# Twelve tiles instead of four leave PSUM by ACT and get tokens and bias by accumulating transfers

## The chip, the core and the metric

The kernel runs on one core of one Trainium2 chip. The metric is the device time of one execution in microseconds (us), median of several. A profile is one further execution, recorded by the hardware profiler; its span runs from the first to the last recorded instruction. The engines of a core are PE (matmul), PEld (its weight loads), DVE (vector), ACT (scalar), POOL and SP; each runs its own queue of instructions in order, and DMA transfers are issued from SP's, ACT's and POOL's queues.

## What is computed

x holds 64 batches of 64 tokens by 1024 features. Each batch has a condition, which picks one of 16 matrices of 64x64; the matrix mixes the 64 rows of the batch. On the result a feed-forward layer acts: a base product with a 1024x1024 weight and a bias, plus a low-rank product of 8 experts of rank 16, of which a gate picks the best two. The input is added at the end.

```
W = weights[condition]
h = einsum('bct,bcd->bdt', x, W)
gate_logits = einsum('bsd,ed->bse', h, gate_w)
weights, selected = top_k(gate_logits, 2);  weights = softmax(weights)
result = einsum('bsd,od->bso', h, base_w) + base_b
low = einsum('bsd,erd->ebsr', h, lora_A)
lora_out = einsum('ebsr,eor,bse->bso', low, lora_B, w_full)
return x + result + 2.0 * lora_out
```

## The kernel before

**Tiles.** The 4096 token rows are 32 tiles of 128 rows, two batches each. The condition matrix mixes rows only and the weights mix columns only, so the kernel multiplies by the weights first and by the condition matrix afterwards. The columns of the joined weight (128 of lora_A, 8 of the gate, 1024 of the base) are three chunks, c = 0, 1, 2, of 384, 388 and 388 columns. The 1024 rows of the weight are four blocks of 256, so that the blocks are named b11 to b43 (row block, then chunk).

**Precision.** Every operand is split into a rounded high part and the rest, and each product is three matmuls: high by high, high by rest, rest by high. The high part is a copy (L234, mostly on ACT): wh of the weights, xh of x, zh of the products, bdh of the condition matrix, lth of the transposed low-rank part. The rest is a subtraction on DVE (L231): wl, xl, zl, bdl, ltl. The subtraction needs the copy, and the matmuls need both.

**Plain tiles and pairs.** Tiles 0 to 3 are multiplied block by block (`plain`): for tiles 0 and 1, row block by row block as the weights arrive, chunks 0 and 1 of both tiles, then chunk 2. Tiles 4 to 31 go in pairs through a scheme with 20 products p1 to p20 in place of 24, on sums and differences of blocks (`Pair.product`), with PSUM banks z0 to z3. The products' matmuls are L414.

**After a product chunk.** `post` brings the chunk z of a tile through the condition matrix: matmuls with bdh and bdl into a bank a0 or a1 (chunk 0) or o0 or o1 (L447). The condition matrix of a tile comes by a gather from HBM, issued from POOL (`load_cond`, L394, tile bdr), and is then split by ACT into bdh and by DVE into bdl. Chunk 0 also feeds the gate (copy low, then small steps L486 to L493 on DVE and ACT) and a transpose of the weighted low-rank part on PE (L500), which is split into lth and ltl; three more matmuls by lora_B add it to every chunk.

**The end of a tile.** `finish` takes each of the three chunks out of PSUM into the tile's buffer xtok, of which there are three, used in turn (tile i uses i % 3). For tiles from 4 on the buffer already holds x + bias, and DVE adds the bank to it (L457). That is the work of `load_tok`: SP loads the tile's x (L380), then POOL issues a transfer of the bias that accumulates onto it (L381). For tiles 0 to 3 ACT copies the bank into the buffer (L234), and `late_sum` afterwards issues from POOL two accumulating transfers onto it, x and then the bias (L388). The store is issued from POOL for tiles 0 to 29 (L464). A transfer onto a buffer waits for the landing of the one before; that wait stands in the issuing engine's queue.

**Order.** No engine's order is written out by hand. Each step is registered with `add`, with the engine, a cost, what it reads and writes, and for matmuls a due time. `Program.run` works back from the due times along the dependences to a latest start of each step (`late`), and then plays the program forward on its costs; whenever an engine is free it takes, among the steps that are ready by that reckoning, the one with the earliest latest start. A DMA enters with its issue, 2.0 us, and its bytes at 360 GB/s, one after another; an accumulating transfer counts 2.5 times its bytes, a gather the 64 KB of its matrix. The order found in this way is then fixed in the queues, whatever the chip's own times are. So a change of what one step costs or waits for can move any other step on any engine.

**The start.** 39 small matmuls on zeros (L225) keep PE busy until the first weights are there. ACT and DVE split the weight blocks (wh_b.., wl_b..) and the x blocks of tiles 0 and 1 (xh, xl) as SP's loads land. The indices of the conditions come by a POOL DMA (L223), POOL makes rows of them (L593), and then issues the first two gathers.

Of the kernel before, what the change touches and what calls it, by code (L numbers as in the profile page):

```python
# [36 lines left out]
NPAIR = NT // 2  # L37
NPLAIN = 2
TOP = 3.0e38
NWARM = 39  # L40

PE, ACT, DVE, POOL, SP = "PE", "ACT", "DVE", "POOL", "SP"
# [37 lines left out]
class Program:  # L80
# [7 lines left out]
    def add(self, engine, cost, fn, reads=(), writes=(), due=None, first=False, size=0.0, early=None, port=False,  # L88
            after=0.0):

        n = len(self.steps)
        engine, cost = (e if isinstance(e, (list, tuple)) else [e] for e in (engine, cost))
        deps = set()
        for b in list(reads) + list(writes):
            if b in self.writer:
                deps.add(self.writer[b])
        for b in writes:
            deps.update(self.readers.get(b, ()))  # L100
        for b in reads:
            self.readers.setdefault(b, []).append(n)
        for b in writes:
            self.writer[b], self.readers[b] = n, []
        deps.discard(n)
        self.steps.append(dict(eng=dict(zip(engine, cost)), fn=fn, deps=deps, first=first, size=size, port=port,
                               lag=FLIGHT + QUEUE + size * DMA if size else 0.0, after=after,
                               due=self.horizon if due is None else due,
                               early=SP in engine and not reads if early is None else early))
# [59 lines left out]
def cond_ffn_kernel(ctx, tc, xT, x, idx, cw, wall, bias, lb, out):  # L169
# [50 lines left out]
    for t in low:  # L220
        nc.vector.memset(t[:, NG:], TOP)
    idx_sb = sb.tile([P, NT], I32, name="idx_sb")
    nc.gpsimd.dma_start(idx_sb, idx)  # L223
    for _ in range(NWARM):
        nc.tensor.matmul(bank["o1"][:, :P], wz, wz, start=True, stop=True)  # L225
# [7 lines left out]
    def copy(e, o, a):  # L233
        (nc.scalar.copy if e == ACT else nc.vector.tensor_copy)(o, a)  # L234
# [139 lines left out]
    def tok_keys(j):  # L374
        return [("xtok", j, str(c)) for c in (0, 1, 2) + PARTS]

    def load_tok(i):
        j = i % 3
        keys = tok_keys(j)
        add(SP, ISSUE, lambda e: nc.sync.dma_start(xtok[j], x[i * P:(i + 1) * P, :]), writes=keys, size=4.0 * T * P)  # L380
        add(POOL, 1.1, lambda e: nc.gpsimd.dma_start(xtok[j], bias.broadcast_to([P, T]), accum_op=ALU.add),  # L381
            writes=keys, size=TWICE * 4.0 * T * P)

    def late_sum(i):

        j = i % 3
        for src in (x[i * P:(i + 1) * P, :], bias.broadcast_to([P, T])):
            add(POOL, 1.1, lambda e, src=src: nc.gpsimd.dma_start(xtok[j], src, accum_op=ALU.add),  # L388
                writes=tok_keys(j), size=TWICE * 4.0 * T * P)

    def load_cond(i):

        j = i % 2
        add(POOL, 1.04, lambda e: nc.gpsimd.indirect_dma_start(  # L394
            out=bdr[j], out_offset=None, in_=cw,
            in_offset=bass.IndirectOffsetOnAxis(ap=rows[:, i:i + 1], axis=0)),
            ["rows"], [("bdr", j)], size=4.0 * P * P, early=True)
        add(ACT, 0.28, lambda e: copy(e, bdh[j], bdr[j]), [("bdr", j)], [("bdh", j)])
        add(DVE, 0.25, lambda e: sub(e, bdl[j], bdr[j], bdh[j]), [("bdr", j), ("bdh", j)], [("bdl", j)], port=True)
# [19 lines left out]
    def split_z(n, src, key):  # L419

        q = take("zq", NZ)
        h, l = zh[q][:, :n], zl[q][:, :n]
        add(ACT, 0.2 + 0.00085 * n, lambda e: copy(e, h, src()), [key], [("zh", q)])
        add(DVE, 0.09 + 0.00104 * n, lambda e: sub(e, l, src(), h), [key, ("zh", q)], [("zl", q)],
            port=isinstance(key, tuple))
        return q

    def outs(c):

        c, p = c if isinstance(c, tuple) else (c, slice(0, CN[c]))  # L430
        lo, o, n = max(OUTS[c][0] - p.start, 0), OUTS[c][2] + max(p.start - OUTS[c][0], 0), p.stop - p.start
        return n, slice(lo, n), slice(o, o + n - lo), p
# [18 lines left out]

    def finish(i, c, b):
        (_, s, o, _), j = outs(c), i % 3
        if i < 2 * NPLAIN:
            return add(ACT, 0.2 + 0.00085 * (s.stop - s.start), lambda e: copy(e, xtok[j][:, o], bank[b][:, s]),
                       [b], [("xtok", j, str(c))])
        add(DVE, 0.09 + 0.00104 * (s.stop - s.start), lambda e: nc.vector.tensor_tensor(  # L457
            xtok[j][:, o], bank[b][:, s], xtok[j][:, o], ALU.add), [b], [("xtok", j, str(c))])

    def store(i, cs):  # L460
        o, j = slice(outs(cs[0])[2].start, outs(cs[-1])[2].stop), i % 3
        src = [("xtok", j, str(c)) for c in cs]
        if i < NT - 2:
            add(POOL, 1.0, lambda e: nc.gpsimd.dma_start(out[i * P:(i + 1) * P, o], xtok[j][:, o]), src,  # L464
                size=4.0 * P * (o.stop - o.start))
        else:

            q, dma = (ACT, nc.scalar.dma_start) if cs[0] == PARTS[1] else (SP, nc.sync.dma_start)
            add(q, ISSUE, lambda e: dma(out[i * P:(i + 1) * P, o], xtok[j][:, o]), src,
                size=4.0 * P * (o.stop - o.start))  # L470
# [37 lines left out]
    def post(i, c, q):  # L508

        if c == 0:  # L510
            b = held[i] = f"a{i % 2}"
            if i >= NT - 2:
                pr.horizon -= SOONER
            sums(i, 0, b, q, (0, 1, 2), start=True)
            gate(i, b)
            tr(i, b)
            sums(i, 0, b, with_lora=True, stop=True)
            finish(i, c, b)
            if i >= NT - 2:
                pr.horizon += SOONER  # L520
            return
        else:
            b = f"o{take('o', 2)}"
            if i >= NT - 2:
                parts = [(c, b)] if (i, c) != (NT - 2, 2) else list(zip(PARTS, (b, "z3")))
                for c, b in parts:
                    sums(i, c, b, with_lora=True, start=True)
                for c, b in parts:
                    sums(i, c, b, q, (0, 1, 2), stop=True)
                    finish(i, c, b)  # L530
                return
            else:
                sums(i, c, b, q, (0, 1, 2), True, True, True)
        finish(i, c, b)
# [8 lines left out]
    t = 4.9  # L543
# [168 lines left out]
    class Pair:  # L712
# [29 lines left out]
        def chunk(self, i, c, o=None):  # L742

            t = 2 * self.q + i
            if o:
                u = self.at[o]
                post(t, c, split_z(CN[c], lambda: unit(u)[:, :CN[c]], ukey(u)))
                sts.give(u)
            else:
                post(t, c, split_z(CN[c], lambda: bank[BANKS["X"]][:, :CN[c]], BANKS["X"]))  # L750
            self.out.add((i, c))
            if self.q == NPAIR - 1:
                for p in PARTS if (i, c) == (0, 2) else (c,):
                    store(t, (p,))
            elif all((i, c) in self.out for c in range(3)):
                store(t, range(3))

        def product(self, p):
# [49 lines left out]
    def load_pair(q):  # L808
        for i in (2 * q, 2 * q + 1):
            load_cond(i)  # L810
            load_tok(i)

    pairs = {}
    for q, p in ORDER:
        pr.horizon = ends[q] + (LAST if q == NPAIR - 1 else LAG)
        if q not in pairs:
            pairs[q] = Pair(q)
        if (q, p) == (NPLAIN, HEAD[3]):
            load_pair(q)
        pairs[q].product(p)  # L820
        if p == TAIL[-1] and q < NPAIR - 1:

            load_pair(q + 1)
# [40 lines left out]
```

## Time and profile before

| | |
|---|---|
| median of 3 runs | 460.26 us (460.14 to 460.26) |
| profiled execution: time | 460.46 us |
| its span | 458.7 us |
| granted PE clock | 1.0 throughout |
| DMA moved | 75.00 MB, mean 164 GB/s |
| accumulating transfers among them | 32 of bias (28 at L381, 4 at L388) and 4 of x |

The profile's page opens with the busy time of each engine, its share of the span and its instructions. Its 40 slices of the span show busy tenths:

```
PE   8999999999999999999999999999999999999995
DVE  5999997879989788796987979798797988888674
ACT  5864666543736345373543646354454544546331
POOL 3030214121303021220303003030210403103000
```

Further views are asked of the trace: a list of waits (who waited for whom, total, times, longest), a timeline (start, length, engine, line, operation, tiles, and in brackets the idle time before it and what ended it), the busy times of each engine in stretches of time, and the DMA issues with their size and the median time from issue to landing. In names, the text before "<-" is what is written. Numbers of buffers and blocks are left out there, so that wh_b_b is the high part of any weight block used plainly; which one it is follows from the order.

### The profile page before, as it was taken

The numbers are of one execution on the slowest core, as the hardware profiler recorded it, in microseconds if no ns is written. First come the engines' busy times: TensorE is split into PE (matmuls) and PEld (weight loads), VectorE is DVE, ScalarE is ACT, GpSimd is POOL, SyncE is SP. The second block draws the span as 40 slices with busy tenths as digits, with TensorE's granted clock in tenths as the row PEclk, the third lists the DMA queues.
The fourth block names the chain that finished last, engine by engine and source line by source line (L and its number), as shares of the span: only waits on it lengthen the run. The fifth ranks groups of instructions, "written<-read, shape, count | busy, mean of one in ns | idle before, by whom it ended". The sixth has DMA issues, their size and how long they took to land.

```text
span 458.7 us, 7577 instructions
## 1 busy us (share of the span) xinstructions
PE 452.7 (99%) x2621; PEld 449.7 (98%) x2621; DVE 383.5 (84%) x941; ACT 227.2 (50%) x520; POOL 89.6 (20%) x107
## 2 busy tenths in 40 slices
PE   8999999999999999999999999999999999999995
PEld 8999999999999999999999999999999999999995
DVE  5999997879989788796987979789797988888674
ACT  5864666543736345373543646354454544546331
POOL 3030214121303021220303003030210403103000
PEclk9999999999999999999999999999999999999999
DMA  8932748977768462764847456565565746556142
GB/s 279 352 117 47 153 107 198 213 211 202 180 206 202 172 161 87 217 131 163 199 127 202 108 182 148 172 162 133 191 123 185 173 129 193 116 174 149 51 134 91
DMA packets 36229, 75.00 MB, mean 164 GB/s; under 512 B 4432, under 2 KB 22240, under 8 KB 36192
## 3 DMA queue, kind: packets, MB, share of 16 engines
q0 software_dynamic: 10560, 36.72, 33.5%
q1 hardware_dynamic: 25200, 37.32, 25.9%
q10 hardware_dynamic: 432, 0.49, 0.4%
q8 instruction: 20, 0.33, 0.3%
q14 instruction: 17, 0.14, 0.1%
HBM read 57.74 MB, written 16.78 MB: 162 GB/s over the span
## 4 chain that ended last, share of the span: by engine, by line
PE 97%; DMA 1%; DVE 1%; ACT 0%; issue 0%
PE ps_z L414 76%; PE ps_o L447 15%; PE ps_a L447 6%; DMA w_b<-in_w 1%; PE ps_a L500 1%; DVE wl_b_b L231 0%; DVE xtok L457 0%; DVE st L740 0%; ACT wh_b_b L234 0%; DVE xl L231 0%; PE ps_z L447 0%; DVE xh L234 0%
## 5 line engine op out<-in xcount | busy, mean ns | idle before, releaser
L231 DVE TENSOR_TENSOR xl<-xr,xh 128x512 fp32r<-128x512 f32 (+1 forms) x138 | 92.1, 670 | 20.0 <-ACT xh L234 19.8
L414 PE MATMUL ps_z<-wh_t_p,xh 128*128 128x388 f32 (+1 forms) x308 | 105.3, 342 | 0.1
L414 PE MATMUL ps_z<-wh_t_p,xl 128*128 128x388 f32 (+1 forms) x308 | 104.3, 339 | 0.0
L414 PE MATMUL ps_z<-wl_t_p,xh 128*128 128x388 f32 (+1 forms) x308 | 104.3, 339 | 0.0
L234 ACT CAST xh<-xr 128x512 fp32r<-128x512 f32 (+1 forms) x136 | 82.5, 610 | 37.2 <-PE ps_z L414 32.5
L740 DVE TENSOR_TENSOR st<-ps_z,st 128x388 f32<-128x388 f32 x126 | 70.2, 558 | 21.2 <-PE ps_z L414 20.2
L292 DVE TENSOR_TENSOR xr<-xr 128x256 f32<-128x256 f32 (+1 forms) x139 | 69.6, 526 | 3.6 <-DMA xr<-in_xT 3.4
L414 PE MATMUL ps_z<-wh_b_p,xh 128*128 128x388 f32 (+1 forms) x180 | 61.4, 341 | 0.0
L414 PE MATMUL ps_z<-wh_b_p,xl 128*128 128x388 f32 (+1 forms) x180 | 60.9, 338 | 0.0
L414 PE MATMUL ps_z<-wl_b_p,xh 128*128 128x388 f32 (+1 forms) x180 | 60.8, 338 | 0.0
L414 PEld LDWEIGHTS ps_z<-wh_t_p,xh 128*128 128x128 f32 x308 | 57.8, 188 | 1.2 <-DVE st L740 0.7
L414 PEld LDWEIGHTS ps_z<-wl_t_p,xh 128*128 128x128 f32 x308 | 57.9, 188 | 0.0
L414 PEld LDWEIGHTS ps_z<-wh_t_p,xl 128*128 128x128 f32 x308 | 57.9, 188 | 0.0
L464 POOL DMA_DIRECT2D out<-xtok x30 | 16.8, 560 | 193.6 <-DVE xtok L457 89.6
L234 ACT CAST zh<-st 128x388 fp32r<-128x388 f32 (+1 forms) x70 | 36.1, 517 | 22.1 <-DVE st L740 15.2
L381 POOL DMA_DIRECT2D xtok<-in_bias x28 | 27.0, 964 | 96.9 <-DMA xtok<-in_x 89.6
L394 POOL DMA_INDIRECT bdr<-in_cw,rows x32 | 36.9, 1155 | 26.4 <-DVE zl L231 17.7
L457 DVE TENSOR_TENSOR xtok<-ps_o,xtok 128x388 f32<-128x388 f32 (+1 forms) x56 | 30.9, 554 | 11.2 <-PE ps_o L447 10.7
L723 ACT ACTIVATE ps_z<-ps_z 128x388 f32<-128x388 f32 x42 | 20.1, 478 | 40.5 <-PE ps_z L414 39.4
L231 DVE TENSOR_TENSOR zl<-st,zh 128x388 fp32r<-128x388 f32 (+1 forms) x70 | 38.7, 554 | 0.9 <-ACT zh L234 0.6
L414 PEld LDWEIGHTS ps_z<-wh_b_p,xh 128*128 128x128 f32 x180 | 33.8, 188 | 0.2
L414 PEld LDWEIGHTS ps_z<-wl_b_p,xh 128*128 128x128 f32 x180 | 33.8, 188 | 0.0
(143 smaller groups left out, 873.0 us busy)
## 6 DMA issues: line engine op xcount, KB each, us to landing
xr<-in_xT SPq DMA_DIRECT2D x128, 128.0 KB, 3.2
xtok<-in_bias POOLq DMA_DIRECT2D x32, 512.0 KB, 7.1
out<-xtok POOLq DMA_DIRECT2D x30, 512.0 KB, 3.2
xtok<-in_x SPq DMA_DIRECT2D x28, 512.0 KB, 3.6
w_b<-in_w SPq DMA_DIRECT2D x10, 388.0 KB, 5.9
xtok<-in_x POOLq DMA_DIRECT2D x4, 512.0 KB, 6.6
out<-xtok SPq DMA_DIRECT2D x3, 194.0 KB, 2.2
bdr<-in_cw,rows POOLq DMA_INDIRECT x32, 5.3
```

Of the source, the lines that this page charges most:

```text
L231: eng[e].tensor_tensor(o, a, b.bitcast(F32), ALU.subtract)
L234: (nc.scalar.copy if e == ACT else nc.vector.tensor_copy)(o, a)
L292: add(DVE, tt_cost(2 * P * len(os)), lambda e: nc.vector.tensor_tensor(some(xr, os), some(xr, xs), some(xr, ys), f), [("xr", u) for u in s ...
L381: add(POOL, 1.1, lambda e: nc.gpsimd.dma_start(xtok[j], bias.broadcast_to([P, T]), accum_op=ALU.add), writes=keys, size=TWICE * 4.0 * T * P)
L394: add(POOL, 1.04, lambda e: nc.gpsimd.indirect_dma_start(out=bdr[j], out_offset=None, in_=cw, in_offset=bass.IndirectOffsetOnAxis(ap=rows[ ...
L414: nc.tensor.matmul(z, l[:, j, n], w.ap()[:, f, :cols], start=(start and q == 0), stop=(stop and q == 2), skip_group_check=True)
L447: nc.tensor.matmul(d, l, r, start=(start and m == 0), stop=(stop and m == len(mms) - 1), skip_group_check=True)
L457: add(DVE, 0.09 + 0.00104 * (s.stop - s.start), lambda e: nc.vector.tensor_tensor(xtok[j][:, o], bank[b][:, s], xtok[j][:, o], ALU.add), [ ...
L464: add(POOL, 1.0, lambda e: nc.gpsimd.dma_start(out[i * P:(i + 1) * P, o], xtok[j][:, o]), src, size=4.0 * P * (o.stop - o.start))
L500: add(PE, 0.107, lambda e: nc.tensor.matmul(tp, low[i % 2][:, :ER], ident, is_transpose=True, start=False, stop=False, skip_group_check=True),
L723: add(ACT, 0.2 + 0.00085 * W, lambda e: nc.scalar.mul(z[b], z[x], scale), [BANKS[x]], [BANKS[b]])
L740: add(DVE, 0.09 + 0.00104 * W, lambda e: nc.vector.tensor_tensor(unit(u), a(), b(), f), reads, [ukey(u)])
```

## The change

A new constant LATE = 12 replaces 2 * NPLAIN = 4 as the bound in `finish`; the pairs call `late_sum` ahead of the store of a tile below it; and `load_pair` leaves `load_tok` out for such a tile. So tiles 4 to 11 are treated at their end as tiles 0 to 3 are. Tiles 12 to 31 keep the old way.

```diff
+LATE = 12
...
     def finish(i, c, b):
         (_, s, o, _), j = outs(c), i % 3
-        if i < 2 * NPLAIN:
+        if i < LATE:
             return add(ACT, 0.2 + 0.00085 * (s.stop - s.start), lambda e: copy(e, xtok[j][:, o], bank[b][:, s]),
                        [b], [("xtok", j, str(c))])
...
             elif all((i, c) in self.out for c in range(3)):
+                if t < LATE:
+                    late_sum(t)
                 store(t, range(3))
...
     def load_pair(q):
         for i in (2 * q, 2 * q + 1):
             load_cond(i)
-            load_tok(i)
+            if i >= LATE:
+                load_tok(i)
```

Since the planner settles the order, instructions that the diff does not name stand at other places in the queues too: on PE from about 24 us on (its last 700-odd instructions stand as before), on ACT and DVE from about 9 us on, on SP from about 13 us on, and on POOL from the fifth gather on.

## The prediction

> **What bounds the kernel now.** I read the page's busy shares first, then the busy time by stretches, then the list of waits of PE alone, and only then the timelines of single engines at the places where the change reorders work. The busy shares and two of the stretches:
>
> ```profile
> span 458.7 us, 7577 instructions
> PE 452.7 (99%) x2621; PEld 449.7 (98%) x2621; DVE 383.5 (84%) x941; ACT 227.2 (50%) x520; POOL 89.6 (20%) x107
> ...
> 12.00:40.00 28.00, 28.00 (x162) 27.85 (x161) 27.79 (x54) 18.05 (x37) 3.50 (x2) 1.00 0.57 191
> ...
> 240.00:420.00 180.00, 180.00 (x1039) 179.41 (x1038) 151.71 (x384) 87.45 (x206) 37.07 (x41) 1.00 0.60 161
> ```
>
> In the stretches the columns are length, sum, then PE, PEld, DVE, ACT and POOL busy. From 12 to 420 us PE is busy for the whole of every stretch. A busy PE alone proves little, since its matmuls overlap, but starts support it: two 384-column matmuls start 0.17 to 0.18 us apart, and outside the first 12 and the last 20 us I find no gap over 0.1 us between starts beyond that pace. PE's list of waits holds one entry, at the very start:
>
> ```profile
> PE ps_o L225 <- DVE warm L311: 1.1, 1, 1.1
> ```
>
> Two things follow. Freeing DVE, ACT or POOL in the middle gains nothing: PE has no idle time to give back there; what is left is about 0.7 us near 440 to 447 us, where it waits for DVE st L740, and the order of PE's last 700-odd instructions is the same in the changed program. And any stall of PE is lost for good, because no later slack absorbs it. So the question is only whether the new order makes PE wait anywhere.
>
> **The change, part by part: eviction.** Tiles 4 to 11 have three evictions each. DVE loses 16 of 0.554 us (L457, ps_o) and 8 of 0.405 us: 12.1 us. ACT gains 16 copies of 0.483 and 8 of 0.374 us: 10.7 us, on an engine that is half idle. Cost and gain at the end of the chain: 0, covered by PE's own work on both sides. If ACT's cover were gone, a copy would cost at most its 0.48 us.
>
> **The token transfers.** SP loses eight issues of 0.33 us; POOL gains eight of 0.92 us (the median at L388), a total of 7.4 us on an engine with 20% busy. What matters is the chain behind the last eviction of a tile, in POOL's queue: tokens, then bias onto them, then the store, each waiting for the landing of the last. The DMA view gives:
>
> ```profile
> xtok<-in_bias POOLq DMA_DIRECT2D x32, 512.0 KB, 7.1
> out<-xtok POOLq DMA_DIRECT2D x30, 512.0 KB, 3.2
> xtok<-in_x SPq DMA_DIRECT2D x28, 512.0 KB, 3.6
> xtok<-in_x POOLq DMA_DIRECT2D x4, 512.0 KB, 6.6
> ```
>
> That is 6.6 + 7.1 + 3.2 = 16.9 us until the buffer is free, where before the store, the plain load and the bias took 3.2 + 3.6 + 7.1 = 13.9 us between the same two evictions. The Trainium skill ("DMA: Bandwidth & Descriptors", Anatomy of one DMA) gives a transfer on this path about 2.0 us plus its bytes at 436 GB/s, which makes 3.2 us for 512 KB and 9.6 us for the chain; the rows, which accumulate, say twice that for two of the three, and I use the rows. Where is it felt? With three buffers, the second tile of a pair (t7, t9, t11, evicted first) reuses the buffer of the first tile of the pair before (t4, t6, t8, evicted last). Walking POOL's new order with the positions of the sums in PE's new order (at PE's pace, no stall): t4's last eviction near 103 us, its tokens land at 110, its bias at 117, its store at 120.5; t7's first eviction is ready near 123. For t6 to t9 it is 148 against 151, for t8 to t11 175.5 against 178. A slack of 2.5 to 3 us each. Two accumulations under way at once took up to 9 us (around 75 us). With 9 us each the store lands at most 2 us after the eviction is ready, and what waits behind it in ACT's queue, the copy lth of the other tile, is wanted by PE only 2.2 us or more after that point. Value taken: 0; bounds 0 and about 2 us over the three places. Then t13, which loads the old way again behind t10's late store, cannot get its bias before about 213 us; the new order puts its DVE additions behind the sums of the next pair, near 221, so 0 again. Tiles 0 to 3 already run this path in the profile, without a wait of PE.
>
> **The order of the start.** All engines' orders come from a planner, and the eight accumulations lengthen the chain that it works back from. So it moves up the work of the first tiles. ACT's program before and after, from the end of the third weight block (listing, not profile; the names are those of the code):
>
> ```
> before: wh b21, xh, wh b22, xh, wh b31, xh, wh b32, xh, wh b41, xh, bdh0, wh b42
> after:  wh b21, xh, bdh0, wh b22, xh, wh b31, xh, bdh1, wh b32, xh, wh b41
> ```
>
> bdh0 is the copy of the first gathered condition matrix. ACT runs its queue in order, so everything behind it now waits for that gather. On DVE, bdl0 moves up too, ahead of wl b22. POOL's and SP's first issues are the same as before, so the gather comes when it came:
>
> ```profile
> 6.87 1.06 POOL L394 DMA_INDIRECT bdr<-in_cw,rows  x1 [0.18 <-issue]
> ...
> bdr<-in_cw,rows POOLq DMA_INDIRECT x1, 5.9
> ...
> 8.91 0.40 ACT L234 CAST xh<-xr 128x256 fp32r<-128x256 f32 x1
> 9.46 0.84 ACT L234 CAST wh_b_b<-w_b 128x776 fp32r<-128x776 f32 x1
> 10.21 0.40 ACT L234 CAST xh<-xr 128x256 fp32r<-128x256 f32 x1
> ...
> 10.34 0.97 DVE L231 TENSOR_TENSOR wl_b_b<-w_b,wh_b_b 128x776 fp32r<-128x776 f32 x1
> 11.22 0.42 DVE L231 TENSOR_TENSOR xl<-xr,xh 128x256 fp32r<-128x256 f32 x1
> ...
> 11.69 0.44 PE L414 MATMUL ps_z<-wh_b_b,xl 128*128 128x384 f32 x1
> ```
>
> The first row is its issue, the second its time to landing (POOL's DMA issues between 6 and 8 us); then ACT, DVE and PE where the change strikes. It lands at 6.87 + 5.9 = 12.8 us. ACT is free for bdh0 at 8.91 + 0.40 = 9.3. The steps: bdh0 starts at 12.8; in the profile ACT's next instruction started 0.29 us after it (15.12 to 15.41), so wh b22 starts at 13.1 instead of 9.46: 3.6 us late. xh of the second tile follows at 13.8 instead of 10.21, wl b22 on DVE at 13.9 instead of 10.34 (bdl0, 0.27 us, is done by then: hidden), xl at 14.8 to 15.3 instead of 11.22 to 11.64. PE is already at the limit here: in the profile its matmul on xl starts at 11.69, 0.05 us after xl ends, the last of three that use the second tile's block at 11.28, 11.46 and 11.69. It will run dry at about 11.3, get two of them at 14.2 and the third at 15.3. Loss: 15.3 - 11.7 = 3.6 us. It is not made up: PE is full from 12 us on, and what lies behind (DVE 27.79 of 28 us busy) is moved as a whole. ACT wins back its 1.2 us of waits for weights, which now lie ready, against 0.29 us for bdh1, whose gather (issued 8.23) has landed by then. The late weight block b23, whose load waits for a freed buffer, moves with the rest.
>
> The gather's price from both sides: the 32 gathers took 2.5 to 7.3 us to land, so 0 to 5.0 us of stall. By the skill's formula 64 KB would take 2.15 us, land at 9.0, and bdh0 would cost nothing but its 0.29 us. I take 5.9, because it is this very gather, at this place, with the weights' loads around it (they too took 5 to 6 us). The skill also speaks of the PE clock ("TensorE: Matmul & The Clock Gate", The HAM clock gate): about 3.4 us idle halve it. The trace shows only the price: the 39 warm-up matmuls start 107 ns apart for the first 3.9 us, so getting warm again would cost about half of that, 2 us. The expected hole is 14.2 - 11.3 = 2.9 us, under that figure: 0 taken, 2 the upper end.
>
> **Sum.** The profiled execution took 460.46 us, its span 458.7 and 1.8 around it. Span after: 458.7 + 3.6 = 462.3. The median of the runs, 460.26, is 0.2 below the profiled execution; on it, 460.26 + 3.6 = 463.9.
>
> **Rivals.**
> - The hole lets PE's clock fall: 463.9 + 2 = 465.9. For: 2.9 us is near 3.4. Against: it is below, and two matmuls come before the rest of it. 0.13.
> - Late transfers take over: buffers come free after their evictions, ACT waits with lth behind it, and PE stalls at t7, t9, t11 as well: 0.5 to 2 us more, about 465. For: accumulations of 9 us were seen. Against: the slack of 2.5 to 3 us, and tiles 0 to 3. 0.13.
> - Not slower: the gather lands before ACT gets to bdh0. Place: ACT's queue at 9.3 us; price: nothing below a landing time of 2.5 us, less than the 0.2% bound (0.9 us, about what a measurement of this kernel can tell from no change) below some 3.3 us. Then the time is 460.3 to 461.2, since PE's bound stands. For: gathers of 2.5 us exist. Against: those were on quiet queues; the two near the start took 5.9 and 5.4. 0.06, of which 0.01 for faster: by more than 0.9 us it cannot be from PE's remaining gaps, which are about 0.7 us.
> - The forecast, 463.9, itself 463.0 to 464.7 with the gather 0.8 us either way: 0.68.
>
> The range 463.0 to 466.0 takes in the cold clock and most of the late transfers.
>
> **What would show it.** In the changed profile, ACT's bdh has idle time of about 3.4 us before it, released by the DMA bdr, near 12.8 us; PE has a hole of about 3 us before 14.3, released by ACT xh, and a smaller one before 15.3, released by DVE xl; from there to 440 us it is full again, and everything lies 3.6 us later. Matmuls 0.35 us apart after the hole would be the cold clock. Waits of ACT xtok for DMA out near 127, 155 and 182 us, with PE idle after them, would be late transfers. Wrong it is if the gather comes early, or if PE has some slack at 12 us that the trace does not show.

## The result and the profile after

The changed kernel takes **467.35 us** (median of 6 executions, 464.76 to 470.52) against 460.26 us (460.14 to 460.76): a ratio of 1.015 [1.0132, 1.0168], slower by 7.1 us. The forecast was 463.9, with 466.0 as its upper end. The executions of the kernel before lie within 0.6 us; those of the changed one spread over 5.8 us. Part of what happens below is thus different from one execution to the next. The profiled execution was the shortest, 464.76 us with a span of 462.9.

First the page of the changed kernel and its stretches, with the columns as before (length, sum, PE, PEld, DVE, ACT, POOL, granted clock, share of the DMA engines, GB/s):

```profile
span 462.9 us, 7579 instructions
PE 454.3 (98%) x2621; PEld 450.8 (97%) x2621; DVE 373.1 (81%) x917; ACT 234.5 (51%) x544; POOL 94.9 (21%) x115
...
12.00:40.00 28.00, 26.14 (x138) 25.78 (x139) 25.79 (x50) 18.10 (x36) 2.22 (x2) 0.94 0.55 186
212.00:228.00 16.00, 16.00 (x96) 15.98 (x95) 13.65 (x30) 5.90 (x12) 1.46 (x2) 1.00 0.63 169
```

DVE has 10 us less to do, ACT 7 more, and neither shows in the time. In the stretch from 12 to 40 us two things changed: PE has 1.86 us of idle time, where it had none, and the granted clock is 0.94, where it was 1.00. From 212 to 228 us, a place that matters below, PE is full in this execution. PE's list of waits names what it waited for:

```profile
PE ps_z L415 <- ACT wh_b_b L235: 2.5, 1, 2.5
PE ps_o L226 <- DVE warm L312: 1.1, 1, 1.1
PE ps_z L415 <- DVE xl L232: 0.4, 1, 0.4
```

The middle entry was there before. The two others are new, once each. The timelines of ACT and of PE around that place follow, each in a fence of its own (start, length, engine, line, operation, tiles, and the idle time with its releaser). They answer to the rows near 9 to 12 us shown of the kernel before.

```profile
8.48 0.40 ACT L235 CAST xh<-xr 128x256 fp32r<-128x256 f32 x1
12.05 0.30 ACT L235 CAST bdh<-bdr 128x128 fp32r<-128x128 f32 x1 [3.17 <-DMA bdr<-in_cw,rows]
12.26 0.83 ACT L235 CAST wh_b_b<-w_b 128x776 fp32r<-128x776 f32 x1
```

```profile
10.64 0.34 PE L415 MATMUL ps_z<-wh_b_b,xl 128*128 128x384 f32 x1
13.45 0.44 PE L415 MATMUL ps_z<-wh_b_b,xh 128*128 128x384 f32 x1 [2.47 <-ACT wh_b_b L235]
...
14.48 0.44 PE L415 MATMUL ps_z<-wh_b_b,xl 128*128 128x384 f32 x1 [0.41 <-DVE xl L232]
...
15.66 0.52 PE L415 MATMUL ps_z<-wh_b_b,xl 128*128 128x388 f32 x1
15.99 0.53 PE L415 MATMUL ps_z<-wh_b_b,xh 128*128 128x388 f32 x1
```

The first fence and the upper lines of the second are the step that the prediction made: ACT stands at the gather (3.17 us), the weight copy behind it comes late, and so does PE; DVE's xl ends at 14.4, and PE's next start follows at 14.48. Beyond PE's usual pace of 0.175 us from start to start, the hole is 2.6 us at 13.45 and 0.6 at 14.48. Not all of this is loss against the kernel before, since PE came to the hole 0.46 us sooner in this execution (10.64 against 11.10 for the same matmul): behind the hole it is 2.8 us late (14.48 against 11.69).

The last two lines are what the prediction had put at nothing: matmuls of 388 columns that start 0.32 us apart instead of 0.18. Ten of them do, which is 1.5 us. The granted clock, third from the end of each row, is a half over just these matmuls and full in the stretch before them:

```profile
12.18:15.59 3.41, 1.73 (x8) 1.41 (x9) 2.76 (x5) 3.41 (x8) 0.95 (x1) 1.00 1.04 383
15.59:19.01 3.42, 3.42 (x13) 3.42 (x12) 3.42 (x6) 2.58 (x6) 0.00 (x0) 0.50 1.05 372
```

The hole and the slow matmuls make PE 4.3 us late, which is the whole difference of the spans (462.9 against 458.7).

So the shortest execution is explained by the start. The median is 2.6 us longer; for that, another execution is needed (e4 below).

### The profile page after: what moved, and what is told of

Same layout as the page of the kernel before. It is cut to its first block, busy times and chain, and to the rows that moved or that the text cites. A ratio compares the mean times of both kernels' runs of the same rounds, so it can differ in the third digit from the quotient of the medians.

```text
span 462.9 us, 7579 instructions
## 1 busy us (share of the span) xinstructions
PE 454.3 (98%) x2621; PEld 450.8 (97%) x2621; DVE 373.1 (81%) x917; ACT 234.5 (51%) x544; POOL 94.9 (21%) x115
## 2 busy tenths in 40 slices
DMA packets 36230, 75.01 MB, mean 162 GB/s; under 512 B 4432, under 2 KB 22240, under 8 KB 36192
## 4 chain that ended last, share of the span: by engine, by line
PE 96%; DMA 2%; issue 0%; DVE 0%; ACT 0%; POOL 0%; POOLq 0%; DVEq 0%
PE ps_z L415 74%; PE ps_o L448 15%; PE ps_a L448 6%; DMA bdr<-in_cw,rows 1%; DMA idx_sb<-in_idx 1%; PE ps_a L501 1%; ACT wh_b_b L235 0%; DVE xtok L458 0%; DVE st L741 0%; DVE xl L232 0%; POOL rows L594 0%; POOL ident masks.py:199 0%; PE ps_z L448 0%; ACT bdh L235 0%; POOL ident masks.py:197 0%
## 5 line engine op out<-in xcount | busy, mean ns | idle before, releaser
L395 POOL DMA_INDIRECT bdr<-in_cw,rows x32 | 35.5, 1108 | 33.5 <-ACT e L489 17.7
L415 PEld LDWEIGHTS ps_z<-wh_b_p,xl 128*128 128x128 f32 x180 | 33.8, 188 | 0.0
L382 POOL DMA_DIRECT2D xtok<-in_bias x20 | 19.4, 972 | 67.1 <-DMA xtok<-in_x 57.9
```

What stands on the lines that cost most here:

```text
L395: add(POOL, 1.04, lambda e: nc.gpsimd.indirect_dma_start(out=bdr[j], out_offset=None, in_=cw, in_offset=bass.IndirectOffsetOnAxis(ap=rows[ ...
L415: nc.tensor.matmul(z, l[:, j, n], w.ap()[:, f, :cols], start=(start and q == 0), stop=(stop and q == 2), skip_group_check=True)
```

## The experiments

Most experiments leave the planner's order as it is and move single instructions. For that, the planned steps are first collected and then issued, with a list of moves in between; "bdh0" and the like are names given to single steps. Line numbers in these kernels are larger by the lines added. A gap of PE is counted here as the time between two starts beyond the usual pace.

```diff
-            steps[i]["fn"](e)
+            seq.append((i, e))
...
+        for e, tag, before in MOVES:
+            new = next(q for q in seq if steps[q[0]]["tag"] == tag)
+            seq.remove(new)
+            seq.insert(next(n for n, q in enumerate(seq) if steps[q[0]]["tag"] == before), new)
+        for i, e in seq:
+            steps[i]["fn"](e)
```

**e1, the two early copies put back in the changed kernel.**

```diff
+MOVES = ((ACT, "bdh0", "wh_b42_0"), (DVE, "bdl0", "zl_0"))
```

> The changed kernel with two instructions put back: ACT's copy bdh0 stands where it stood before the change (after five more weight and x copies), and DVE's bdl0 stands ahead of zl of the first product chunk. Every other instruction of every engine keeps the changed kernel's order. Theory A, all of the loss comes from the start (ACT held by the first gather, then PE's clock): 460.3 us, within 0.5, and a spread as small as before's. Theory B, the accumulating transfers of tiles 4 to 11 cost something in the middle as well, above all in the longer executions: 462 us or more, with a spread of 2 us or more.

Measured: 466.07 us, 1.0128 [1.0096, 1.0159]. This experiment was badly made. In the changed order POOL had already issued the gather of tile 2 into the same buffer, and the moved copies stood behind it: they waited for that later gather, and tile 0 used tile 2's matrix. PE has gaps of 1.5 us near 25.6 and 0.9 near 30.5 us in place of the hole. It says nothing on the start. It does show, in an execution without a hole at 13 us, gaps of 0.5 and 1.0 us at 220.3 and 223.5. e5 mends it.

**e2, the two early copies alone, in the kernel before.**

```diff
+MOVES = ((ACT, "bdh0", "wh_b22_0"), (DVE, "bdl0", "wl_b22_0"))
```

> The kernel before, with only the same two instructions moved the other way: ACT's bdh0 ahead of the copy wh of b22, DVE's bdl0 ahead of wl of b22. No token transfer is changed. Theory A: the whole loss appears, median 466 to 468 us, with a spread from 464.7 to 470 as in the changed kernel. Theory B: only what the profiled execution shows at the start, about 464.8 us, with a small spread.

Measured: 464.53 us (464.17 to 465.33), 1.0097 [1.0083, 1.0112]. PE's list of waits has the same two new entries as that of the changed kernel, and beside them only the one for warm:

```profile
PE ps_z L427 <- ACT wh_b_b L246: 2.4, 1, 2.4
...
PE ps_z L427 <- DVE xl L243: 0.4, 1, 0.4
```

Two instructions moved, with PE's own order untouched, cost 4.4 us, with a spread of 1.2 us: a hole of 2.6 + 0.6 us and, in the profiled execution, eleven matmuls at half pace. The start is thus one cause, and in these four executions not one that spreads over 6 us.

**e3 and e4, the hole filled with work of PE, and the changed kernel once more beside it.**

```diff
+NFILL = 44
...
+    def fill(e):
+        for _ in range(NFILL):
+            nc.tensor.matmul(bank["o1"][:, :P], wz, wz, start=True, stop=True)
+    MOVES[:] = [(PE, fill, ("plain", 1, 0, 1, 0))]
```

> The changed kernel with 44 small matmuls on zeros put into PE's queue ahead of the matmul that waits at 11 us (some 55 ns each at full clock, 2.4 us in all), so that PE is busy through most of the hole. If the falling clock costs as the profile shows (ten matmuls 0.146 us late each): 1.5 us less than the changed kernel in its shortest executions, 463.3 us. If the spread of the executions is the clock's (more or fewer periods at half clock): median 463 to 465, spread below 2 us. If the spread comes from the gather's landing: the median falls by 1.5 to 2 us only, and executions up to 468 us remain.

> The changed kernel again, unaltered, for a profile of another execution and for more times beside the others on the same chip: 464.8 to 470.5 us, median about 467. If the profile falls on a longer execution, theory A has it landing the first gather later than 12 us or running longer at half clock after the hole; theory B has gaps of PE between 100 and 330 us.

Measured: the filled kernel 464.41 us (463.45 to 465.23), 1.0094 [1.0081, 1.0107]; the changed kernel again 466.68 (465.29 to 469.55), 1.0149 [1.0118, 1.018]. The filler does not make PE's real work start earlier, since the weight copy is as late as before; what it is there to change is the clock. It takes off 2.3 us, and the spread falls to 1.8 us. The mean granted clock of every execution moves with it: 0.991 to 0.996 in all six of the changed kernel, 0.991 to 1.000 in e4, 0.995 to 0.996 in e2, but 0.997 to 0.999 in e3, and 0.998 to 1.000 in the kernel before on that chip.

How to read this mean: in every profile the clock falls to half again at the very end, 2 us or more behind the start of the last matmul (in e3 from 459.8 us on, with the last start at 457.8). That takes up to 0.003 off the mean and costs PE nothing; it is all that is missing in the profile of e3. One stretch at half clock in full work, 3.4 us as above, takes off 0.0037. A mean of 0.991 thus holds more than one such stretch; no trace kept shows where a second one lies.

One minus the clock, times the span, is 3.3 us at the median of the changed kernel (0.993), 2.3 at that of e4 (0.995) and 0.9 at that of e3 (0.998). By this count the filler saves 1.4 us against e4 and 2.4 against the first six executions. The 2.3 us timed against e4 may therefore hold more than the clock. The spread does as well: with this count taken off, the twelve executions of the changed kernel still reach from 462.5 to 467.2 us. The profiled execution of e4, with a clock of 0.998, shows the hole and no matmul at half pace, so not every hole costs it.

That execution of e4 took 467.43 us, and shows the second cause. Two stretches of the kernel before, the same two of e4, and what is new in PE's list of waits:

```profile
80.00:95.00 15.00, 15.00 (x87) 14.96 (x87) 12.65 (x35) 8.73 (x21) 4.10 (x5) 1.00 0.94 235
212.00:228.00 16.00, 16.00 (x93) 16.00 (x93) 13.05 (x36) 7.10 (x18) 4.62 (x5) 1.00 0.68 188
```

```profile
80.00:95.00 15.00, 14.13 (x79) 13.27 (x79) 10.70 (x29) 6.63 (x17) 3.65 (x4) 1.00 0.44 108
212.00:228.00 16.00, 14.69 (x84) 14.03 (x84) 11.68 (x25) 5.01 (x11) 1.89 (x2) 1.00 0.65 165
```

```profile
PE ps_z L415 <- DVE st L741: 1.8, 3, 0.9
...
PE ps_z L415 <- ACT ps_z L724: 0.4, 1, 0.4
```

PE is idle near 87 to 93 and near 222 to 225 us, released by DVE st and ACT ps_z, the steps that pass the partial sums on. Gaps there: 0.4 + 0.75 and 0.6 + 1.05, together 2.8 us. What kept DVE is on its timeline:

```profile
215.93 0.28 DVE L232 TENSOR_TENSOR bdl<-bdr,bdh 128x128 fp32r<-128x128 f32 x1
219.23 0.42 DVE L293 TENSOR_TENSOR xr<-xr 128x256 f32<-128x256 f32 x1 [3.02 <-DMA xr<-in_xT]
...
222.32 0.43 DVE L293 TENSOR_TENSOR xr<-xr 128x256 f32<-128x256 f32 x1 [1.27 <-DMA xr<-in_xT]
```

DVE stands for 3.02 us and again for 1.27 us at sums of x blocks of the next pair, because their loads (SP, issued from 212.75 on) have not landed; the sums st that PE needs (220.50 and 223.26) stand behind them in DVE's queue. Near 84 us it is the same, 2.89 us. In the shortest execution the first of these waits near 216 us is 0.68 us and that near 83 us 1.22, and PE does not feel them. Of the places that the prediction's rival named, near 127, 155 and 182 us, none shows a gap in any execution profiled.

**e5, the start put back rightly.** The gather of tile 2 moves behind the two copies as well.

```diff
+MOVES = ((ACT, "bdh0", "wh_b42_0"), (DVE, "bdl0", "zl_0"), (POOL, "gather2", "gather3"))
```

> The changed kernel with its start put back in a right order: bdh0 on ACT stands ahead of the second half of the fourth weight row's copy, bdl0 on DVE ahead of the first split of the softmax result, and on POOL the gather of tile 2 behind them, ahead of that of tile 3. Nothing else moves. Theory (start and middle are two separate losses): PE is full from 12 us to at least 80 us, and what is left over the kernel before is the middle alone, 0 to 5 us and different from execution to execution: median 461.5 to 463.5, with waits of DVE for x blocks near 80 and near 215 us. Rival (the middle is only upset because PE comes late out of the start): 460.3 to 460.8, small spread.

Measured: 464.82 us (463.80 to 465.42), 1.0095 [1.0082, 1.0109], above what either theory expected. The hole and the half pace are gone. PE's waits, without that for warm:

```profile
PE ps_z L429 <- DVE st L755: 0.8, 1, 0.8
PE ps_z L429 <- DVE wl_b_b L245: 0.7, 1, 0.7
PE ps_z L429 <- ACT ps_z L738: 0.3, 1, 0.3
PE ps_z L429 <- DVE zl L245: 0.2, 1, 0.2
```

The first and third are the middle, at 221 and 218 us. The second and fourth, gaps of 0.9 and 0.3 us near 28 and 23 us, are a third cause: with these three instructions put back, the rest of the changed order in the first 30 us still costs 1.2 us. In the two profiles of the changed kernel itself that place shows at most 0.2 us; there PE comes to it 3.4 to 4.3 us late already. The middle does not need the late start.

**e6 to e8, what keeps the x loads.** All three are e5 with transfers left out: the plain token load of tile 13 that lies among the x loads near 210 us; the late bias of tiles 4 to 11; both late transfers of these tiles.

```diff
-        add(SP, ISSUE, lambda e: nc.sync.dma_start(xtok[j], x[i * P:(i + 1) * P, :]), writes=keys, size=4.0 * T * P)
+        add(SP, ISSUE, lambda e: nc.sync.dma_start(xtok[j], x[i * P:(i + 1) * P, :]) if i != 13 else None, writes=keys, size=4.0 * T * P)
```

```diff
-        for src in (x[i * P:(i + 1) * P, :], bias.broadcast_to([P, T])):
+        for n, src in enumerate((x[i * P:(i + 1) * P, :], bias.broadcast_to([P, T]))):
+            go = lambda e, src=src: nc.gpsimd.dma_start(xtok[j], src, accum_op=ALU.add)
+            if 4 <= i < LATE and n == 1:
+                go = lambda e: None
```

In e8 the condition is shorter:

```diff
+            if 4 <= i < LATE:
```

> As the kernel with its start put back, without the plain token load of tile 13 by SP, near 209 us (tile 13 then lacks its tokens). Theory A (the stall near 215 to 225 us comes from that load lying among the loads of x blocks): DVE's wait for x near 215 us falls under 0.5 us and PE's stalls near 220 are gone, 1 to 2 us below the kernel with its start put back in the longer executions; the place near 80 to 90 us is unchanged. Rival B (the accumulating transfers alone crowd the DMA engines): the wait for x and the stalls stay, same time within 0.5 us.

> As the kernel with its start put back, without the late bias transfers of tiles 4 to 11 (these tiles then lack their bias); all other instructions keep their order. Theory A (the added transfers hurt by the traffic and by the length of the chain): stores end some 7 us sooner, SP's wait for a buffer near 195 us is gone, tile 13's load moves ahead of the x loads, and PE's stalls near 220 us vanish: 460.3 to 461.3, with what is left near 80 to 95 us, where tiles 2 and 3 still have their transfers. Rival B (DVE's new order itself frees the x blocks too late): DVE's wait near 215 us and PE's stalls stay, 461.5 to 463.5.

> As the kernel with its start put back, without both late transfers, tokens and bias, of tiles 4 to 11 (these tiles then hold the evicted sums alone); all other instructions keep their order. Theory A (traffic and chain): PE full in the middle, 460.3 to 460.8, small spread. Rival B (order alone): as the kernel with its start put back, 461.5 to 463.5. If the stall near 90 us stays and the one near 220 us goes, the first is of the order and of tiles 2 and 3, the second of the added transfers: about 461.

Measured: without tile 13's load 466.75 us, 1.0126 [1.0111, 1.0141], longer by 1.9 us; without the late bias 463.03, 1.006 [1.0047, 1.0073]; without both 462.87, 1.0061 [1.0044, 1.0078]. In the last two PE has no gap near 220 us. Both stay above the 460.3 to 461.3 us that their theories expected: the third cause stays, and in the profile of e8 a gap of 0.75 us near 90 us. The DMA issues of the stretch in which the x loads of the next pair are sent (KB of each, median us from issue to landing) say why. Of e5, of e6, of e7, and of the kernel before:

```profile
xr<-in_xT SPq DMA_DIRECT2D x7, 128.0 KB, 6.6
xtok<-in_bias POOLq DMA_DIRECT2D x1, 512.0 KB, 6.7
```

```profile
xtok<-in_bias POOLq DMA_DIRECT2D x2, 512.0 KB, 7.1
xr<-in_xT SPq DMA_DIRECT2D x7, 128.0 KB, 8.0
```

```profile
xr<-in_xT SPq DMA_DIRECT2D x7, 128.0 KB, 4.4
```

```profile
xr<-in_xT SPq DMA_DIRECT2D x7, 128.0 KB, 2.4
```

The seven loads take 2.4 us where nothing lies beside them, 4.4 beside a plain token load (e7, that of tile 13, 4.7 us to landing), 6.6 beside that and an accumulating bias transfer, and 8.0 beside two accumulating ones. Taking tile 13's load away does harm because its bias transfer no longer waits for it and starts 6.5 us sooner, beside that of tile 14. Single landings of e6, listed from the trace (issue and landing in us):

```
bias, accumulating:  209.92 to 215.43   210.52 to 219.26
x loads:             211.15 to 215.74   211.53 to 219.54   212.04 to 221.13   212.82 to 221.40
```

The first x load lands 0.3 us after the first accumulation, the second 0.3 us after the second, and the others behind it. DVE waits 5.03 us for them, and PE has a gap of 2.6 us at 222. In e7 no late bias delays the stores, and tile 14's bias transfer has ended (201.6 to 206.7) before the x loads start at 209.2; in e5 it runs from 208.43 to 215.12, and the first x load, sent at 209.21, lands at 215.32. A plain transfer holds them up in the same way: in e7 the token load of tile 13 runs from 210.13 to 214.83, and the x load sent behind it at 210.56 lands at 215.19. So the late transfers do not hurt by being late for their own buffer. They push the next tiles' bias into the moment at which the x loads are sent.

**e9 and e10, the place near 80 us, and what it is about the transfers.** e9 leaves out tile 2's late bias too; e10 is e5 with all late transfers as plain copies.

```diff
+            if i in (2, 4, 5, 6, 7, 8, 9, 10, 11) and n == 1:
+                go = lambda e: None
```

```diff
-            add(POOL, 1.1, lambda e, src=src: nc.gpsimd.dma_start(xtok[j], src, accum_op=ALU.add),
+            add(POOL, 1.1, lambda e, src=src: nc.gpsimd.dma_start(xtok[j], src),
```

> As the kernel without late bias for tiles 4 to 11, and without that of tile 2 too (tiles 2 and 4 to 11 then lack their bias). Theory A (a load of x issued while an accumulating transfer runs lands only behind it; near 74 us it is tile 2's bias): the x load of about 75 us lands within 3 us instead of 5.6 to 7.6, DVE's wait near 80 us falls from 1.6 to 2.5 us to under 0.4, no gap of PE from 31 to 440 us, time 461.9 to 462.5, spread under 1 us. Rival B (DVE's order alone makes it wait there): wait and stalls stay, 463.0 as without the late bias of 4 to 11.

> The changed kernel with its start put back, and all late transfers of tiles 0 to 11 as plain copies of the same size instead of accumulating ones (these tiles then hold the bias alone); order and bytes as before. Theory A (what crowds the x loads out is the accumulation): each late transfer lands in 3 to 4.5 us instead of 5 to 10, x loads beside them in under 5 us, DVE's waits for x near 80 and 215 us fall under 1 us, PE's gaps there are gone, 461.9 to 462.6. Rival B (number and bytes of the transfers): 464.8 as with the start put back.

Measured: 461.86 us, 1.0045 [1.0032, 1.0059], and 462.08, 1.0046 [1.0033, 1.006]. In e9 the x load of about 74.8 us lands in 2.3 us (in e5 5.6, in e6 7.6), and DVE has no wait for x near 80 us; what is left in PE's list beside warm is the third cause, DVE wl_b_b with 0.7 us and DVE zl with 0.2.

Tile 2's transfer was late in the kernel before as well. It is the new order that puts it ahead of an x load that DVE needs soon. e10 moves the same bytes in the same order as e5 (75.01 MB in both). The row of the late token transfers in the DMA view of the whole kernel, of e5 and of e10:

```profile
xtok<-in_x POOLq DMA_DIRECT2D x12, 512.0 KB, 5.5
```

```profile
xtok<-in_x POOLq DMA_DIRECT2D x12, 512.0 KB, 3.7
```

A late token transfer takes 5.5 us accumulating and 3.7 us plain. With that the waits for x near 80 and 215 us are gone (one of 1.4 us near 244 costs PE 0.25), and the x loads of the stretch at 209 us take 4.0 us:

```profile
xr<-in_xT SPq DMA_DIRECT2D x7, 128.0 KB, 4.0
```

The number of transfers and their bytes are thus not enough for the loss; it needs the accumulation. What the accumulation adds is time: plain transfers end sooner, and so do the chains. Tile 14's bias, which accumulates in e10 too, is sent at 204.02 us there, and no longer just ahead of the x loads (208.43 in e5). Whether an accumulating transfer also holds up a load beside it more than a plain one of the same length, this run cannot tell.

**e11, both causes away, and e12, the clock by itself.** e11 is the changed kernel in its own order, with the first matrix loaded plainly at the very start and with plain late transfers. e12 is e2 with the filler of e3.

```diff
+    nc.gpsimd.dma_start(bdr[0], cw[0:P, :])
     nc.gpsimd.dma_start(idx_sb, idx)
...
-        add(POOL, 1.04, lambda e: nc.gpsimd.indirect_dma_start(
+        add(POOL, 1.04, lambda e: None if i == 0 else nc.gpsimd.indirect_dma_start(
```

> The changed kernel in its own order everywhere, the early copies included, but with the first condition matrix loaded by a plain transfer as POOL's first instruction in place of the first gather (tile 0 then uses the wrong matrix) and with the late transfers of tiles 0 to 11 as plain copies (these tiles then hold the bias alone). Theory (the wait for the gather and the accumulation are all there is): no hole at 13 us, no stalls near 85 and 220 us, 460.3 to 461.6. Rival (the new order of ACT and DVE costs by itself, as the 1.2 us of gaps near 23 and 28 us in the kernel with its start put back would have it): 461.6 to 463.

> The kernel before with bdh0 and bdl0 alone moved ahead, as in the run of the early copies alone, and with 44 small matmuls on PE in the hole this makes. Theory A (in most executions the hole lets the clock fall to half for some 3.3 us): 1.3 to 1.6 us below the 464.5 of the early copies alone, so 463.0. Rival B (the clock falls only in some of the executions): 463.6 to 464.5, with single executions near 463.

Measured: e11 461.67 us (461.38 to 461.96), 1.0035 [1.0021, 1.0049], with one gap over 0.2 us between 12 and 440 us:

```profile
PE ps_z L429 <- DVE wl_b_b L245: 0.7, 1, 0.7
```

With neither the gather nor the accumulation in the way, the spread of 6 us shrinks to 0.6, and of 7.1 us 1.6 are left, at the border of the two expectations. In the profile PE is 1.2 us late at 43 us, which is the third cause, and 1.1 us at the end. The rival was right that the order costs by itself. e12: 463.57 us, 1.0071 [1.0058, 1.0085], 1.0 us below e2, with clocks of 0.997 to 1.000 where e2 had 0.995 to 0.996. The time is at the lower end of what rival B expected, but the clocks of e2 (0.995 to 0.996) speak for a stretch at half clock in all its executions. The two kernels were timed on different chips; by the ratios to the kernel before the difference is 1.2 us, and their intervals just touch. So the half clock by itself is shown, at 1.0 to 1.2 us here and at most 2.3 in e3 against e4.

No version came out under the kernel before, and none was to be expected: PE has nothing to win back there.

## Why the prediction was wrong in size

The direction and the first mechanism were right; 3.4 us of the 7.1 were missing. Two terms that the prediction put at 0 failed: the clock and the late transfers.

- **Eviction, 0: right.** e10 and e11 evict tiles 4 to 11 by ACT, and PE has no gap over 0.3 us from 30 to 440 us.
- **The gather, 3.6 us: right, and 0.2 to 0.8 too high.** ACT waited 3.17 us for it (3.4 expected). Behind the hole PE is 2.8 us late in the shortest execution, 3.0 in e2 and 3.4 in e4 (starts at 14.48, 14.65 and 15.10, against 11.69). The gather took at most 5.6 us (issue at 6.42, ACT's copy at 12.05), against 5.9 taken from the row, and not the 2.15 that an estimate by the formula of the Trainium skill ("DMA: Bandwidth & Descriptors", Anatomy of one DMA) makes of its bytes. The row was the better guide. The rest of the difference is the issue itself, at 6.42 to 6.95 us in these executions.
- **The clock, "0 taken, 2 the upper end": failed.** I had weighed an expected hole of 2.9 us against the 3.4 us of the skill ("TensorE: Matmul & The Clock Gate", The HAM clock gate) and let the rule decide. The hole was even shorter, 2.6 us, and the granted clock fell all the same: in all six executions of the changed kernel it is 0.991 to 0.996, and in four of the six of e4 0.995 or less. One stretch at half clock cost 1.5 us in the profile; the clock's whole share at the median is 1.4 to 2.4 us. The rival with the low clock should have been the forecast, and its 2 us the middle of its range and not the end: the price of getting warm again was known from the start of the trace, only the threshold was not.
- **The late transfers, 0 with bounds 0 to 2, and "t13 … so 0 again": failed.** At the three places that I had worked out, buffers t7, t9 and t11, the evictions wait for PE alone in the profiles. The slack was less sure than I had it, though: in the shortest execution t4's store lands at 126.46 us, and t7's first eviction starts at 127.30. I had followed each transfer to those who wait for its own buffer. I had not asked which other transfers are sent while it runs. The x loads of the next pair are sent just then, twice, and land behind the accumulation. DVE waits for them (3.02 us in e4), and PE for what is queued behind in DVE. In the profile of before the rows were there: an x load sent at 76.5 us took 9.6 us beside accumulating transfers, and DVE then waited for x no longer than 0.3 us before 100 us, since its order wanted that block later. At the median this is the rest of the 7.1 us, about 1.3 to 2.9 us; in single executions it is 0 (the shortest) or 2.8 (e4's profile). With the start put back it is 2.3 us (1.0095 less 1.0045, of 460.3). Why it is larger there, and why executions differ, is open: the difference lies in when transfers land, and no run here controls that.
- **The order of DVE and ACT behind the hole, "moved as a whole": nearly right.** It costs 1.2 us by itself (e5, e9, e11), of which the profiles of the changed kernel show at most 0.2; the hole covers the rest. Had the gather come early, the forecast's rival "not slower" would have met this instead of 460.3.

In sum for the median of 7.1 us: the hole 2.8 to 3.4 us, the clock 1.4 to 2.4, the late x loads the remainder. The hole is measured, the clock is shown by e3 and e12 with its size known only within this range, and for the remainder e7, e9 and e10 show the cause.

## What to carry to other kernels

When a change adds transfers, look not only at who waits for them but also at which short loads are sent while they run, and at what stands behind the user of those loads in its engine's queue. A planner that works back from due times can turn a change in the middle into a wait at the start: read the order of each queue where a gather or another slow transfer is the source. And where a hole in a full TensorE is expected, price the clock with it, unless a run shows that a hole of that length leaves it alone.

## What the runs showed of the hardware

- A hole of 2.6 us, with a second one of 0.6 us behind it, in full work of PE halved its pace afterwards (388-column matmuls 0.32 us apart instead of 0.18), for 3.4 us in the two profiles that show it; by the mean clock it did so in most executions. With 44 small matmuls in the hole (e3, e12) neither the profiles nor the clocks (0.997 to 1.000) show it. A hole of 2.7 us in e4 left the pace alone, so what decides is open.
- At the places that cost time, the first 128 KB load sent behind an accumulating 512 KB transfer landed 0.2 to 0.3 us behind it, though it came from another queue (e5 at 74.7 and 209.2 us, sent 0.8 us behind the transfer; e6 at 211.2 and 211.5). One sent 0.4 us behind got through first (e5, 100.79 to 103.83 us, beside a transfer from 100.41 to 108.57). Seven such loads took 2.4 us at the median alone, 6.6 beside one accumulating and one plain transfer, 8.0 beside two accumulating ones.
- Accumulating costs a transfer of 512 KB about half as much again: 5.5 us against 3.7 at the median of twelve.
